# A state-space convolution block on one core: the opening's loads, biases, silus and weight folding in another order

## The chip, the cores and the metric

The kernel runs on one core of one Trainium2 chip. The metric is the device time of one execution in microseconds (us); lower is better. Three runs of the kernel before gave 1737.27 us as their median, from 1737.03 to 1740.41.

## The reference, cut to what matters

The input x has 4 images of 128 channels on 96 x 96 pixels. A group norm (32 groups of 4 channels) comes first. The normed image is then read as a sequence in four directions (rows, rows reversed, columns, columns reversed), and each sequence goes through the same layer; the four results are turned back, multiplied by the fuse weights and added to x.

```python
t = _grouped1x1(x, in_proj_w, in_proj_b, G)          # 128 -> 2 x 256 channels
u, gate = (t[:, :HID], t[:, HID:])
u = silu(u)
u = conv_general_dilated(u, dw_w, padding 2, 5 taps, depthwise)
...                                                  # s, a, bb, cc from u; a scan over the sequence
u = u + _conv1x1(cc * hst + ssm_d[None, :, None] * s, ssm_out_w)
u = _grouped1x1(u * sigmoid(gate), mix_w, mix_b, G)
return _conv1x1(u, out_proj_w, out_proj_b)
...
x = x + einsum('oc,bchw->bohw', fuse_w, y) + fuse_b
```

## The kernel before

The sequences are cut into steps of 16 lines; a step has 4 phases (the position modulo 4, called g or r in the code) and 2 directions s, and 256 hidden channels in two halves j. A *pair* is one phase of one step with both directions; `pair(t)` for t below 6 and `pair_on(t)` from there on make up nearly all of the program, 192 pairs in all. Nothing schedules the work: the instructions stand on each engine in the order in which the code is written, and semaphores are put in where one engine needs another's result. So an instruction that waits holds up all that stands behind it on its engine.

`start()` is the opening, before the first pair. It does the following.

- x of the first image comes in pieces into `acc` (`load_x`, L333 to L337). The image is counted in 24 chunks of 384 columns. As each piece lands, VectorE takes the statistics of its chunks (`bn_stats`, L337).
- While that goes on, TensorE runs fillers (L1188), matmuls whose result nobody reads, first three of 512 columns, then smaller ones, each behind a 6-column matmul (L1216) that waits for the statistics of one chunk.
- The generator `stats_first` (L176 to L216) turns the statistics into the norm. `bn_aggr` (L178); a small product over the groups gives the mean; `ex`; another gives the variance; ScalarE takes the square root (L198) and loads the table for silu (L200); L205 scales the input weights to `wn`. One more product and 16 tiny matmuls give the eight bias columns `bn` (L215, L216). Its `yield`s let `start` put other work between.
- `outer` (L1195) multiplies output weights by fuse weights for each of the four directions d and copies them to `w_of` (L1199). `inner` (L1203) multiplies in the mix weights and L1208 scales the result into `w_fin`. GpSimd then adds up `w_of` and `w_fuse` over the directions in place, four additions on L1257, here called **the fold**. Three one-column matmuls (L1281) use the folded weights, and ScalarE makes `b_fin` of them (L1282). The first addition of the fold overwrites the first two directions of `w_of`, so it waits for the first `inner`, which reads them; the third of the L1281 matmuls reads what the fourth addition writes.
- `burst(j, g)` is the input projection of one phase and half: per direction four 32 x 32 matmuls with 385 columns, from `x_in` through `wn` into a PSUM bank. `silus(j, g)` is its two ScalarE activations (L527) into the tile `sil`; memsets of `edges` (L487, L489) follow on VectorE.
- The second half of the hidden channels (j = 1) gets the 5-tap convolution by `taps`, on VectorE (L740, L744). The first half (j = 0) gets it by TensorE: `conv` (weights `band`) and `conv_less` (weights `less`), after which ScalarE copies the result to `u` (L717).
- The last thing in `start` are the three L1281 matmuls and `b_fin`. Then `pair(0)` begins with its `proj`: first the input projection of the next step for one phase (16 matmuls of 385 columns), then 16 matmuls from `u` through `main`, and so on.

PSUM has eight banks. `taps` work in banks 0 and 1; `banks` in `start` names the two banks of each burst; before, `outer` has the banks 0, 1, 4 and 5, one for each direction, and `inner` has 0 and 1.

SyncE's queue issues the loads in this order: ten pieces of x, the tile of output and fuse weights (`shared`, L353), `main` (L330; it holds the input weights that L205 reads), the two tiles `x_in` of the first step (L305), eight small ones for the gates (L323). All its DMAs take turns on eight semaphores, and an issue waits until the DMA that had its semaphore eight issues earlier has landed. So the eight L323 issues tell, one after the other, when the last four pieces of x, `shared`, `main` and the two `x_in` tiles landed (or SyncE came free).

## Time and profile before

| what | value |
|---|---|
| median of three runs | 1737.27 us (1737.03 to 1740.41) |
| profiled execution, first to last instruction (span) | 1735.2 us |
| median less span: what lies around the instructions | 2.07 us |
| TensorE busy in the span | 1713.6 us, 99% |
| VectorE, ScalarE, GpSimd busy | 1507.9, 1494.8, 1447.0 us |
| TensorE's first instruction starts | 11.66 us |
| silus of the opening: first one starts, last one ends | 24.46 us, 32.18 us |
| first matmul of `pair(0)` | 33.71 us |

The page of the profile gives busy times by engine, the chain of work that ended last, and the costliest groups. The timeline lists instructions in order of time, equal ones merged: start, duration of the group, engine, line, operation, output from input, and in brackets how long the engine had been idle and what released it. A matmul in fp32 stands there as two records. The windows give busy time and DMA rate by stretch of time.

### The profile page before, as it was taken

What the parts mean: (1) busy time and instruction counts of PE and PEld (TensorE: products, weight loads), DVE (VectorE), ACT (ScalarE), POOL (GpSimd) and SP (SyncE); (2) the same over time, 40 slices, a digit from 0 to 9 for tenths busy, and PEclk for the clock granted to TensorE, in tenths of its full rate; (3) what the DMA queues carried; (4) which work ended last, traced back from release to release, by engine and by line L of the source; (5) the groups of instructions that cost most, each with busy time, mean ns of one, the idle gap of its engine ahead of it and who ended that gap; (6) DMA issues with size and microseconds to landing.
All of it is one profiled execution on the core that took longest, in us unless ns stands there. A gap on an engine that the chain in (4) does not pass through costs nothing.

```text
span 1735.2 us, 54226 instructions
## 1 busy us (share of the span) xinstructions
PE 1713.6 (99%) x22522; PEld 644.7 (37%) x22522; DVE 1507.9 (87%) x1508; ACT 1494.8 (86%) x2544; POOL 1447.0 (83%) x1490
## 2 busy tenths in 40 slices
PE   7999999999999999999999999999999999999998
PEld 4333333343333433344333443334333333333333
DVE  6899998888889998888889999888888888888887
ACT  4888988889888888888988888888998889888875
POOL 3689889888789988888788988887878889887887
PEclk9999999999999999999999999999999999999999
DMA  7746865358884786337896487433887548643364
GB/s 244 235 147 218 288 202 151 124 206 280 275 287 139 262 267 194 118 126 263 260 308 226 150 300 251 144 123 132 294 294 239 179 144 304 201 137 133 147 226 166
DMA packets 154644, 363.66 MB, mean 210 GB/s; under 512 B 19104, under 2 KB 120864, under 8 KB 154400
## 3 DMA queue, kind: packets, MB, share of 16 engines
q1 hardware_dynamic: 154256, 360.16, 62.8%
q8 instruction: 178, 2.92, 0.7%
q14 instruction: 66, 0.54, 0.1%
q10 hardware_dynamic: 144, 0.04, 0.0%
HBM read 221.41 MB, written 138.53 MB: 207 GB/s over the span
## 4 chain that ended last, share of the span: by engine, by line
PE 95%; DVE 2%; ACT 1%; DMA 1%; issue 0%; SPq 0%; DVEq 0%; ACTq 0%
PE psum L130 81%; PE psum L577 8%; PE psum L557 5%; DVE psum L744 1%; PE psum L1188 0%; DMA acc<-in_xr 0%; DMA kept<-shared 0%; DVE u L638 0%; ACT psum L589 0%; ACT psum L742 0%; DVE u L744 0%; ACT sil L527 0%; SPq L335 0%; PE psum L1195 0%; DVE u L691 0%
## 5 line engine op out<-in xcount | busy, mean ns | idle before, releaser
L744 DVE SCALAR_TENSOR_TENSOR psum<-sil,small,psum 128x768 f32<-128x768 f32 x576 | 589.1, 1023 | 42.2 <-ACT psum L742 16.8
L130 PE MATMUL psum<-u,w_fin 128*32 128x384 f32 (+1 forms) x6192 | 541.3, 484 | 1.1 <-ACT ys L860 0.4
L130 PE MATMUL psum<-u,main 128*32 128x384 f32 x6144 | 535.0, 489 | 0.5 <-DVE u L691 0.4
L638 DVE SCALAR_TENSOR_TENSOR u<-gate,psum 128x768 f32<-128x768 f32 x376 | 341.7, 950 | 150.0 <-PE psum L577 50.8
L879 POOL TENSOR_TENSOR acc<-ys,acc 128x384 f32<-128x384 f32 x375 | 411.8, 1120 | 14.0 <-ACT ys L860 1.9
L825 POOL TENSOR_TENSOR t<-t,t 64x384 f32<-64x384 f32 (+1 forms) x192 | 287.2, 1496 | 70.6 <-DVE t L819 48.3
L589 ACT COPY psum<-u 128x768 f32<-128x768 f32 x384 | 301.4, 799 | 10.5 <-DVE u L638 4.3
L130 PEld LDWEIGHTS psum<-u,w_fin 128*32 128x32 f32 x6192 | 195.2, 109 | 309.6 <-issue 235.5
L130 PEld LDWEIGHTS psum<-u,main 128*32 128x32 f32 x6144 | 180.0, 109 | 324.5 <-issue 218.3
L130 PE MATMUL psum<-sil,band 128*32 128x384 f32 x3072 | 285.3, 488 | 0.0
L792 POOL TENSOR_SCALAR t<-tm 64x384 f32<-64x384 f32 x184 | 170.8, 928 | 114.4 <-ACT tm L781 102.4
L826 POOL TENSOR_TENSOR t<-t,t 64x384 f32<-64x384 f32 (+1 forms) x192 | 233.9, 1218 | 15.1
L793 POOL TENSOR_TENSOR t<-t,tm 64x384 f32<-64x384 f32 x192 | 213.8, 1113 | 30.2 <-ACT t L784 15.5
L577 PE MATMUL psum<-t,main 32*128 32x384 f32 x1536 | 228.1, 525 | 4.2 <-ACT psum L589 4.2
L742 ACT ACTIVATE psum<-sil,small 128x768 f32<-128x768 f32 x191 | 172.6, 904 | 65.2 <-DVE u L638 61.9
L744 DVE SCALAR_TENSOR_TENSOR u<-sil,small,psum 128x768 f32<-128x768 f32 x192 | 194.9, 1015 | 6.8
L527 ACT ACTIVATE sil<-psum,bnorm 128x385 f32<-128x385 f32 x384 | 191.6, 584 | 4.0 <-DMA edge<-sil 0.9
L557 PE MATMUL psum<-x_in,wn 32*128 32x384 f32 x768 | 161.7, 498 | 0.0
L862 ACT COPY ys<-psum 128x384 f32<-128x384 f32 x288 | 132.3, 478 | 33.0 <-PE psum L130 28.3
L130 PEld LDWEIGHTS psum<-sil,band 128*32 128x32 f32 x3072 | 88.8, 108 | 171.4 <-issue 63.1
L781 ACT ACTIVATE tm<-psum,small 128x384 f32<-128x384 f32 x192 | 110.9, 578 | 14.0 <-PE psum L130 2.3
L577 PEld LDWEIGHTS psum<-t,main 32*128 32x128 f32 x1536 | 93.9, 183 | 73.7 <-issue 41.0
(108 smaller groups left out, 1512.3 us busy)
## 6 DMA issues: line engine op xcount, KB each, us to landing
gate<-kept SPq DMA_DIRECT2D x114, 768.0 KB, 5.2
kept<-gate SPq DMA_DIRECT2D x74, 768.0 KB, 3.7
sil<-sil SPq DMA_DIRECT2D x64, 770.0 KB, 6.6
lone<-edge SPq DMA_DIRECT2D x40, 770.0 KB, 7.5
x_in<-in_xs SPq DMA_DIRECT2D x250, 96.2 KB, 3.3
edge<-sil SPq DMA_DIRECT2D x96, 192.5 KB, 3.6
out<-acc SPq DMA_DIRECT2D x46, 384.0 KB, 6.4
acc<-in_xr SPq DMA_DIRECT2D x39, 384.0 KB, 6.4
```

Source lines behind the costliest of these rows:

```text
L130: nc.tensor.matmul(o[r, : rhs.shape[-1]], lhsT, rhs, start=start, stop=stop, skip_group_check=True)
L527: nc.scalar.activation(sils[step][:, s, j, g, :], bank(bk)[:, : N + 1], AF.Silu, bias=bn[:, 1:2] if j else bn[:, 4 + g : 5 + g],)
L557: nc.tensor.matmul(bank(to)[:, :N], stats[un["b"]][0][r, s, :], x_in[s][r, q, off : off + N], start=True, stop=True)
L577: nc.tensor.matmul(bank(ssm(bi, s) + j)[:, :N], w_so[r, bass.ts(j, P)], z[r, :], start=(bi, s) not in seeded, stop=True, skip_group_check= ...
L589: nc.scalar.copy(psum[:, ssm(bi, s) : ssm(bi, s) + 2, :N], us[bi][:, s])
L638: nc.vector.scalar_tensor_tensor(v, g, 1.0, pz, ALU.add, ALU.mult)
L742: nc.scalar.activation(part, src, AF.Copy, scale=w_tap[:, 0:1])
L744: nc.vector.scalar_tensor_tensor(us[i][:, :, 1, :] if k == K - 1 else part, src, w_tap[:, k : k + 1], part, ALU.mult, ALU.add,)
L793: nc.gpsimd.tensor_mul(ta[0:64, p, :], tb[0:64, :], tm[0:64, :])
L825: engine.tensor_mul(ta[0:64, p, r], tb[64:P, r], ta[64:P, p, r])
L826: engine.tensor_add(tb[0:64, r], ta[0:64, p, r], tb[0:64, r])
L879: adder.tensor_add(part, y, part)
```

## The change

Ten things change, all in the opening; every pair after it is as before.

1. x comes in 15 pieces: three of one chunk, nine of two, three of one. Before, it came in ten of 1, 1, 1, 2, 2, 3, 4, 4, 4 and 2 chunks.
2. The fillers read the first 512 columns of x, not columns from chunk 10 on. There are five of 512 columns, then eight of 128, each behind a 6-column matmul on the statistics of one of the last eight chunks.
3. The four first bias columns are made by themselves (L212), ahead of the 16 tiny matmuls, which now write bank 7; the other four come by L217 after another `yield`. The first burst stands between the two.
4. `outer` runs in banks 4 and 5, two directions in each. Only direction 0 goes before the variance; the copies of the other three go to VectorE and stand behind all biases.
5. The bursts and silus of j = 1 come first, then those of j = 0.
6. The banks of the bursts are a ring of three pairs.
7. All taps of the first phase are spread between the silus of j = 1 and j = 0. Before, they lay behind the silus of j = 0.
8. `load_rows` reloads `x_in` for the next step in four issues, not eight.
9. `conv` and `conv_less` come after all silus. Before, they stood among the silus of j = 1.
10. `inner` and the fold come after `conv_less` and the edge DMAs, directly ahead of the L1281 matmuls (L1283 after the change). Before, they stood among the silus.

```diff
-        pb = bank(free[0])
+        pb, pg = bank(7), bank(7)[:, 4:8]
         product(pb[:, 0:4], wn, gm4)
+        nc.vector.tensor_sub(bn[:, 0:4], b_in[:, 0:4], pb[:, 0:4])
+        yield
         for g in range(4):
             for q in range(R):
-                mm(pb[:, 4 + g : 5 + g], q, ..., mean[0:32, :], True, True)
-        nc.vector.tensor_sub(bn, b_in, pb[:, 0:8])
+                mm(pg[:, g : g + 1], q, ..., mean[0:32, :], True, True)
+        nc.vector.tensor_sub(bn[:, 4:8], b_in[:, 4:8], pg[:, 0:4])
...
-    load_x([(0, 1), (1, 1), (2, 1), (3, 2), (5, 2), (7, 3), (10, 4), (14, 4), (18, 4), (22, 2)])
+    load_x([(0, 1), (1, 1), (2, 1)] + [(c, 2) for c in range(3, 21, 2)] + [(21, 1), (22, 1), (23, 1)])
...
-        for n in (512, 512, 512):
-            filler(n)
+        for i in (7, 7, 7, 0, 1):
+            filler(512, i)
         next(pieces)
-        for c, n in ((NSC - 5, 192), (NSC - 4, 192), (NSC - 3, 192), (NSC - 2, 192), (NSC - 1, 256)):
+        for c in range(NSC - 8, NSC):
...
-            filler(n)
+            filler(128)
         next(pieces)
-        outer(0, 0, nc.scalar.copy)
-        outer(1, 1, nc.scalar.copy)
+        outer(0, nc.scalar.copy)()
         next(pieces)
-        outer(2, 4, nc.scalar.copy)
+        copies = [outer(d, nc.vector.tensor_copy) for d in (1, 2, 3)]
         next(pieces)
-        outer(3, 5, nc.vector.tensor_copy)
-        filler(128)
+        sils[0] = new_sil(0)
+        pairs = {1: ((2, 3), (6, 7), (4, 5), (2, 3)), 0: ((6, 7), (4, 5), (2, 3), (6, 7))}
...
+        next(pieces)
+        burst(1, TURN[0])
         for _ in pieces:
             pass
-        for g in range(R):
-            burst(0, g)
+        for copy in copies:
+            copy()
+        burst(1, TURN[1])
+        burst(1, TURN[2])
+        new_u(0)
+        silus(1, TURN[0])
+        taps(0, (0,), nc.vector)
+        burst(1, TURN[3])
+        load_rows(1, slice(0, R))
...
         silus(0, 0)
-        burst(1, TURN[0])
-        silus(0, 1)
-        burst(1, TURN[1])
-        silus(0, 2)
-        inner((0, 1), 0)
-        inner((2, 3), 1)
+        burst(0, 3)
+        load_rows(0, slice(0, R))
+        for g in range(1, R):
+            silus(0, g)
+        conv(0, head_banks(0))
+        conv_less(0, head_banks(0))
+        keep_lone(0)
+        load_lone(0)
+        inner((0, 1), 2)
+        inner((2, 3), 3)
         for w in (w_of, w_fuse):
             for e in (2, 1):
                 nc.gpsimd.tensor_add(w[:, 0:e], w[:, 0:e], w[:, e : 2 * e])
...
         pf = bank(3)
```

The built programs show the places. On TensorE, at the end of the opening, before (`x_in_70` and `x_in_71` are the two directions' inputs, L1203 is `inner`, L1281 the three one-column matmuls that wait for the fold, and the x_in rows behind them are the first of `pair(0)`):

```order
L1203 MATMUL psum<-shared 128x128 x8
L130 MATMUL psum<-x_in_70,wn_269 32x385 x4
L130 MATMUL psum<-x_in_71,wn_269 32x385 x4
L130 MATMUL psum<-x_in_70,wn_269 32x385 x4
L130 MATMUL psum<-x_in_71,wn_269 32x385 x4
L130 MATMUL psum<-sil_299,band 32x384 x8
L130 MATMUL psum<-sil_299,less 32x384 x8
L1281 MATMUL psum<-small,shared 128x1 x3
L130 MATMUL psum<-x_in_70,wn_269 32x385 x8
L130 MATMUL psum<-x_in_71,wn_269 32x385 x8
```

The same place on TensorE after the change (L1205 is `inner`, L1283 the one-column matmuls):

```order
L130 MATMUL psum<-sil_286,band 32x384 x8
L130 MATMUL psum<-sil_286,less 32x384 x8
L1205 MATMUL psum<-shared 128x128 x8
L1283 MATMUL psum<-small,shared 128x1 x3
L130 MATMUL psum<-x_in_70,wn_282 32x385 x8
L130 MATMUL psum<-x_in_71,wn_282 32x385 x8
L130 MATMUL psum<-u_0_1_0_337,main 32x384 x16
```

Between `inner` and the one-column matmuls there stood two bursts, `conv` and `conv_less`; now nothing stands between them. On VectorE, from the bias columns to the first taps, before (L215 and L216 are the biases, L1199 the one copy of `outer` that VectorE had, L1208 the scaling behind `inner`):

```order
L1199 COPY shared<-psum 128x256
L215 TENSOR_TENSOR bnorm_272<-small,psum 128x8
L216 TENSOR_SCALAR bnorm_272<-bnorm_272 128x2
L487 MEMSET sil_299 64x1 x6
L1208 TENSOR_SCALAR w_fin<-psum 128x512 x2
L487 MEMSET sil_299 64x1 x2
L489 MEMSET sil_299 128x2
L740 TENSOR_SCALAR psum<-sil_299,small 128x2x384
```

And on VectorE after the change, from the biases to the scaling behind `inner`, all numbers of lines moved by one or two:

```order
L212 TENSOR_TENSOR bnorm_285<-small,psum 128x4
L217 TENSOR_TENSOR bnorm_285<-small,psum 128x4
L218 TENSOR_SCALAR bnorm_285<-bnorm_285 128x2
L1201 COPY shared<-psum 128x256 x3
L491 MEMSET sil_286 128x2
L742 TENSOR_SCALAR psum<-sil_286,small 128x2x384
L746 SCALAR_TENSOR_TENSOR psum<-sil_286,small,psum 128x2x384 x2
L491 MEMSET sil_286 128x2
L746 SCALAR_TENSOR_TENSOR psum<-sil_286,small,psum 128x2x384
L746 SCALAR_TENSOR_TENSOR u_0_1_0_337<-sil_286,small,psum 128x2x384
L489 MEMSET sil_286 64x1 x8
L1210 TENSOR_SCALAR w_fin<-psum 128x512 x2
```

Three copies now stand behind the biases, and the taps of the first phase stand ahead of the j = 0 memsets and of the scaling. The third burst (banks 4 and 5) waits for the second and third of these copies.

More of the change, by code (lines that the diff above doesn't have):

```diff
@@ L1244, in load_rows @@
                 load_front(1, s, slice(64 * s + 32 * j, 64 * s + 32 * j + 32), r)
-        for g in range(R):
-            burst(0, g)
-        silus(0, 0)
-        burst(1, TURN[0])
-        silus(0, 1)
-        burst(1, TURN[1])
-        silus(0, 2)
-        inner((0, 1), 0)
-        inner((2, 3), 1)
+        next(pieces)
+        burst(1, TURN[0])
+        for _ in pieces:
+            pass
+        for copy in copies:
[7 more added lines that the diff above has]
+        load_rows(1, slice(0, R))
+        silus(1, TURN[1])
+        taps(0, (1,))
+        burst(0, 0)
+        silus(1, TURN[2])
+        taps(0, (2,))
+        burst(0, 1)
+        silus(1, TURN[3])
+        taps(0, (3, 4))
+        burst(0, 2)
+        silus(0, 0)
+        burst(0, 3)
[8 more added lines that the diff above has]
+        inner((2, 3), 3)
         for w in (w_of, w_fuse):
```

44 lines of the change are left out of this document (11 added, 33 removed).

## The prediction

> **What bounds the kernel now.** I read the page first: the engines' busy times.
>
> ```profile
> span 1735.2 us, 54226 instructions
> PE 1713.6 (99%) x22522; PEld 644.7 (37%) x22522; DVE 1507.9 (87%) x1508; ACT 1494.8 (86%) x2544; POOL 1447.0 (83%) x1490
> ```
>
> TensorE is idle for 21.6 us in all. So whatever moves its work of the pairs to earlier or later moves the end by as much, unless an idle stretch takes it up. The change touches only what lies ahead of the pairs; I therefore look for one moment: when TensorE starts its first matmul of `pair(0)`. Next comes the chain of waits (start, length, what); in the opening it runs through TensorE from its first filler on.
>
> ```profile
> 11.66 5.49 PE psum L1188 x6
> ...
> 19.29 0.43 PE psum L1188 x2
> ```
>
> But a TensorE that always has a record may still be paced by others, so I read the timelines of TensorE, VectorE, ScalarE and GpSimd (start, length, group, idle time before it).
>
> ```profile
> 20.30 0.24 PE L130 MATMUL psum<-mv,gmean 128*32 128x1 f32 x8
> 20.48 1.16 PE L1195 MATMUL psum<-shared 128*128 128x128 f32 x8
> 21.56 0.31 PE L130 MATMUL psum<-ex,gmean 128*32 128x1 f32 x16
> ...
> 23.29 0.43 PE L130 MATMUL psum<-mean,wn 32*32 32x1 f32 x32
> 23.56 3.80 PE L130 MATMUL psum<-x_in,wn 32*32 32x385 f32 x96
> 27.29 2.05 PE L1203 MATMUL psum<-shared 128*128 128x128 f32 x16
> ...
> 30.72 1.50 PE L130 MATMUL psum<-sil,band 128*32 128x384 f32 x16
> ...
> 32.95 0.83 PE L1281 MATMUL psum<-small,shared 128*128 128x1 f32 x6
> 33.71 1.28 PE L130 MATMUL psum<-x_in,wn 32*32 32x385 f32 x32
> ```
>
> ```profile
> 18.33 0.81 DVE L178 BATCH_NORM_AGGREGATE mv<-bn 128x2 f32<-128x144 f32 x1
> 20.61 0.16 DVE L183 COPY mean<-psum 128x1 f32<-128x1 f32 x1 [1.48 <-PE psum L130]
> ...
> 21.00 0.22 DVE L187 SCALAR_TENSOR_TENSOR ex<-dev,mv 128x1 f32<-128x1 f32 x1
> ...
> 22.57 0.48 DVE L205 TENSOR_SCALAR wn<-main,inv 128x128 f32<-128x128 f32 x2
> 22.99 0.42 DVE L1199 COPY shared<-psum 128x256 f32<-128x256 f32 x1
> ```
>
> ```profile
> 24.46 7.72 ACT L527 ACTIVATE sil<-psum,bnorm 128x385 f32<-128x385 f32 x16 [0.34 <-PE psum L130]
> ...
> 35.85 0.91 ACT L742 ACTIVATE psum<-sil,small 128x768 f32<-128x768 f32 x1 [0.16 <-DVE u L744]
> ```
>
> ```profile
> 28.59 3.31 POOL L1257 TENSOR_TENSOR shared<-shared 128x512 f32<-128x512 f32 x4 [8.42 <-PE psum L1203]
> ```
>
> From 24.46 to 32.18 us ScalarE sets the pace: 16 silus, 0.48 us apart, without a gap. `inner` (2.05 us) and the fold (3.31 us) lie under them, and the fold ends at 31.90, before TensorE asks for its result at 32.95. From 33.71 on the pairs run.
>
> **The change, part by part.** *The arrival of x and `x_in`.* SyncE's small gate loads tell the landings. The third and fourth are in the first row below; each takes 0.47 us, so the fourth starts at 16.41, when the last piece of x has landed. The eighth, in the second row, starts when `x_in_71` has landed, at 23.18. Behind them stand rates in windows of one microsecond: busy time of five engines, clock, DMA share, GB/s.
>
> ```profile
> 15.43 1.45 SPq L323 DMA_DIRECT2D x_in<-in_xs  x2
> ```
>
> ```profile
> 23.18 0.47 SPq L323 DMA_DIRECT2D x_in<-in_xs  x1
> ```
>
> ```profile
> 3.00:4.00 1.00, 0.00 (x0) 0.00 (x0) 0.47 (x1) 0.00 (x0) 0.84 (x5) 1.00 0.81 244
> ...
> 6.00:7.00 1.00, 0.00 (x0) 0.00 (x0) 0.63 (x2) 0.00 (x0) 0.84 (x3) 1.00 1.06 378
> ...
> 12.00:13.00 1.00, 1.00 (x2) 0.48 (x2) 1.00 (x3) 0.00 (x0) 0.00 (x0) 1.00 1.02 424
> ...
> 14.00:15.00 1.00, 1.00 (x2) 0.34 (x1) 1.00 (x4) 0.00 (x0) 0.00 (x0) 1.00 1.04 419
> ```
>
> A chunk is 0.197 MB. Up to chunk 6 the pieces are the same. Behind it 17 chunks now come as seven pieces of two and three of one, where mostly pieces of four came. At 424 GB/s, the rate while pieces of four moved, 17 chunks take 7.9 us. Pieces of two ran at 378 (6 to 7 us) to 419 (14 to 15 us), pieces of one at 244 with the engines busy 0.81 of the time, so 301. At 419 and 301 the 17 chunks take 8.5 us, at 378 and 301 9.2 us. If size does not matter, nothing is lost; nothing can be gained either, as the same bytes stand ahead of `x_in`. So `x_in` lands 0 to 1.4 us later. I take 0.7, near the 419 of a two-chunk piece with a full queue: the last x at 17.1, `x_in_71` at 23.9.
>
> *The norm.* One `bn_stats` stands behind the last landing; the row of x's tile gives its length.
>
> ```profile
> L337 DVE BATCH_NORM_STATS2 bn<-acc x24: 541/544/561, 3.5 to 17.8; 128x6 f32<-128x384 f32 x24
> ```
>
> Now VectorE is still working off pieces of four when x has landed, and `bn_aggr` starts at 18.33. Then it would start at 17.1 + 0.55 = 17.65 and end at 18.5. The mean's product follows at once: TensorE's fillers, which held it up to 20.30 (VectorE idle 1.48), have been worked through while x came. They now start at about 4 us instead of 11.66 and hide behind the statistics; without that cover the last of them would cost 0.2. From the product to `wn` it is 2.75 us in the row (20.30 to 23.05), less the 0.34 for which the next product waited behind `outer` (21.22 to 21.56): `wn` at 20.9. The six matmuls of `outer` that now follow the variance (0.87 of the row's 1.16) end at about 21.2. TensorE could begin the first burst at 21.4, 2.1 us earlier than 23.56. **But the data is not there**: the burst's second direction needs `x_in_71`, at 23.9. First silu 0.90 behind its burst (23.56 to 24.46): the second silu starts at 24.8, against 24.94. Of 2.1 us, 0.1 is left.
>
> *Biases and copies.* The 16 tiny matmuls (0.43) stand behind that burst; then VectorE makes the other biases (two of 0.16) and three copies of 0.42. Second and third copy end at 25.6 and 26.0. The third burst waits for them, so its silus, the fifth and sixth, start at 26.55 and 27.0 instead of 26.25 and 26.7. I take 0.3 lost, 0 to 0.6 by the landing. The last ten silus follow at 0.48: the silus end at 32.3, against 32.18.
>
> *Taps, banks, reloads.* The taps go under the silus: VectorE has nothing else there. The reload of `x_in` for `pair(0)` can start when the last j = 0 burst is through, about 30.5, and such loads took 4.0 us.
>
> ```profile
> x_in<-in_xs SPq DMA_DIRECT2D x2, 192.5 KB, 4.0
> ```
>
> That is there by 35, well before its use below. I count both at nothing; a later landing shows only beyond 39.
>
> *`conv`, `inner`, the fold.* This is the term that counts. `conv` can start one silu before the last, at 31.85; from its start to the one-column matmuls it took 2.23 us (30.72 to 32.95), so `conv_less` ends at 34.1, 1.15 later than before. Then comes `inner`. The fold started 1.30 us behind `inner`'s start (27.29 to 28.59), so at 35.4, and takes 3.31: 38.7. The third one-column matmul waits for it, and behind it in TensorE's order wait all matmuls of `pair(0)`, 0.28 later (a third of 0.83): **39.0, against 33.71**. Taken apart: 4.9 us between `conv_less` and `pair(0)` instead of 0.76, and 1.15 from what lies ahead. `inner` and the fold lost their cover, the silus, and TensorE, which runs through now, would stand still from 36.1 (end of `inner`) to 38.7. GpSimd's durations are taken from the same four additions.
>
> *What the pairs give back.* ScalarE's first tap waited 0.16 for the taps that are now long done. The ceiling is TensorE's idle time in the first pairs:
>
> ```profile
> 33.70:95.10 61.40, 59.55 (x829) 19.95 (x832) 53.79 (x58) 50.67 (x92) 34.52 (x33) 1.00 0.73 228
> ```
>
> 1.85 us in 61.4. I take 0.5, nearer to the wait that I can name; the ends are 0.16 and 1.85.
>
> **Sum:** +5.3 - 0.5 = +4.8 us on the span of 1735.2: 1740.0. The median is 2.07 above that span, so 1742.1 us. The ends: landing 0 to 1.4 instead of 0.7 (-0.7 to +0.7), copies (-0.3 to +0.3), given back 0.16 to 1.85 (+0.35 to -1.35). All at once give +2.5 to +6.1; two of them rarely add up fully.
>
> **A rule against the change: the clock.** The fillers show it: 3 x 512 columns took 5.49 us in six records, 1.79 ns a column, and later 2 x 192 columns 0.43 us, 1.12 ns. TensorE thus ran slow for its first 5.5 us, though the rows' granted clock (the 1.00 ahead of the DMA share) says 1.00 all along. If the hole of 2.6 us ahead of `pair(0)` made it slow again for 5.5 us, this would cost 5.5 x (1 - 1.12/1.79) = 2.1 us. [...]
>
> **The rivals.**
> 1. *The hole is given back whole by the idle time, 1.85 us, or somewhat more*: +2.5 to +3.4, about 1740.2. For it: "busy" holds modelled ends, so the pairs may have slack that no row shows. Against: VectorE and ScalarE cannot work ahead, as each pair's work on them begins with TensorE's product.
> 2. *Not slower: the pairs are paced by SyncE's chain of loads.* If TensorE in the first pairs in truth follows edge, lone and `x_in` loads, which start at the end of the silus, then its start does not count as long as it is earlier than the loads allow. Silus end at the same time (+0.1), and four reload issues fewer, about 0.42 us each, bring that chain forward by up to 1.7: about 1736.0. It decides if the slack of those loads is over 5 us. Against: TensorE never waits for a DMA between 33.7 and 95.1, and is idle 1.85 us there.
> 3. *The clock falls in the hole*: +2.1, 1744.2.
> 4. *It does not do what it says*: small pieces bring x later by the full 1.4 us, the norm gains 0.1 instead of 0.7, `x_in_71` comes at 24.6: 1742.8.
>
> **How the numbers follow.** The forecast has 0.66, the rivals 0.11, 0.07, 0.09 and 0.07. The forecast's own ends, 1740.4 to 1743.4, hold most of it; to leave out no more than 2 in 10 the range goes from 1739.4 (inside rival 1) to 1744.2 (rival 3). A measurement tells 0.2%, 3.5 us, from no change: the bounds are 1740.7 and 1733.8. Slower: rivals 3 and 4 and nine tenths of the forecast, 0.76. Same: the rest of the forecast, rival 1 and most of rival 2, 0.21. Faster: 0.03.
>
> **What would show it.** In the profile of the changed kernel: `bn_aggr` near 17.7; a burst whose second half starts at about 23.9 with TensorE idle before it, released by the DMA of `x_in`; silus ending near 32.3; the fold's group on GpSimd from 35.4 to 38.7; TensorE idle up to 38.7, released by GpSimd; `pair(0)` at 39.0. The prediction is wrong if `pair(0)` starts by 35, if the pairs behind it draw more than 1.9 us closer than before, or if the first pairs' matmuls run at 1.8 ns a column.

## The result, and the profile after

The changed kernel takes **1748.68 us** (median of 5 executions, 1746.91 to 1749.84) against 1737.27 (5 executions, 1736.70 to 1740.41): a ratio of 1.0062, 95% interval 1.0050 to 1.0074. It is slower, as forecast, but by 11.4 us instead of 4.8, and it lies above the range's end of 1744.2. The busy shares on the page give no hint of the cause, as TensorE stays at 99%; but it is busy 13.4 us longer, with 14 records more, in a span that is 12.6 us longer.

```profile
span 1747.8 us, 54255 instructions
PE 1727.0 (99%) x22536; PEld 653.3 (37%) x22536; DVE 1508.5 (86%) x1511; ACT 1495.9 (86%) x2542; POOL 1447.9 (83%) x1490
```

The windows tell where to look (start:end and length, busy time and count of five engines, then granted clock, DMA share, GB/s). In this profile the clock changes at 7.25, 14.08 and 41.39 us, 6.83 and 27.31 us apart; the borders are these moments and others at multiples of 3.41 us from them.

```profile
7.25:10.66 3.41, 3.05 (x7) 1.02 (x6) 3.16 (x8) 0.00 (x0) 3.10 (x9) 1.00 1.02 393
10.67:14.08 3.41, 0.00 (x0) 0.00 (x0) 3.41 (x9) 0.00 (x0) 0.50 (x2) 1.00 1.03 404
14.09:27.73 13.64, 13.57 (x124) 12.01 (x127) 5.82 (x18) 2.16 (x5) 0.39 (x1) 0.50 0.83 218
27.74:41.38 13.64, 13.41 (x160) 6.36 (x158) 6.74 (x20) 8.40 (x17) 0.00 (x0) 0.50 0.40 109
41.40:44.80 3.40, 2.03 (x19) 1.84 (x17) 1.38 (x2) 0.45 (x1) 2.32 (x3) 1.00 0.30 63
```

From 14.08 to 41.39 us TensorE's granted clock is 0.50. Before, the same column says 1.00 all through the opening, though the first fillers ran slow there by their rate (1.79 ns a column against 1.12 later), as the prediction read. The timeline of TensorE shows what stands ahead of it, and what it does to the steps of the forecast (start, length, engine, line, work; lines in the tail of the code are numbered two higher than before).

```profile
4.31 5.99 PE L1190 MATMUL psum<-acc 128*128 128x512 f32 x10 [4.31 <-DMA acc<-in_xr]
14.16 0.59 PE L1218 MATMUL psum<-bn,acc 128*128 128x6 f32 x2 [3.87 <-DVE bn L339]
...
21.29 0.29 PE L130 MATMUL psum<-mv,gmean 128*32 128x1 f32 x8
...
25.84 0.29 PE L130 MATMUL psum<-gm,wn 128*32 128x4 f32 x8
26.06 0.89 PE L130 MATMUL psum<-x_in,wn 32*32 32x385 f32 x8
...
36.64 2.84 PE L130 MATMUL psum<-sil,band 128*32 128x384 f32 x16 [0.23 <-issue]
39.41 1.53 PE L130 MATMUL psum<-sil,less 64*32 64x384 f32 x16
40.87 2.28 PE L1205 MATMUL psum<-shared 128*128 128x128 f32 x16
44.52 0.61 PE L1283 MATMUL psum<-small,shared 128*128 128x1 f32 x4 [1.37 <-POOL shared L1279]
45.74 0.38 PE L1283 MATMUL psum<-small,shared 128*128 128x1 f32 x2 [0.61 <-POOL shared L1279]
46.05 1.27 PE L130 MATMUL psum<-x_in,wn 32*32 32x385 f32 x32
```

The five fillers of 512 columns run as soon as chunk 0 is there, and are through at 10.3. Then TensorE is idle for 3.87 us, until the statistics of chunk 16. Right behind, at half clock, eight steps of 6 and 128 columns take 0.86 us each and hold the mean's product up to 21.29, though its input was there by 18.3. VectorE, ScalarE and GpSimd show the rest.

```profile
17.50 0.80 DVE L178 BATCH_NORM_AGGREGATE mv<-bn 128x2 f32<-128x144 f32 x1
21.64 0.16 DVE L183 COPY mean<-psum 128x1 f32<-128x1 f32 x1 [3.34 <-PE psum L130]
```

```profile
27.63 1.05 ACT L529 ACTIVATE sil<-psum,bnorm 128x385 f32<-128x385 f32 x2 [2.60 <-PE psum L130]
...
35.96 1.07 ACT L529 ACTIVATE sil<-psum,bnorm 128x385 f32<-128x385 f32 x2 [0.16 <-PE psum L130]
```

```profile
42.40 3.28 POOL L1279 TENSOR_TENSOR shared<-shared 128x512 f32<-128x512 f32 x4 [21.91 <-PE psum L1205]
```

| moment | before | forecast | after |
|---|---|---|---|
| mean's product | 20.30 | 18.5 | 21.29 |
| silus end | 32.18 | 32.3 | 37.03 |
| `conv_less` done, next work of TensorE | 32.95 | 34.1 | 40.87 |
| `pair(0)` | 33.71 | 39.0 | 46.05 |

From there on everything keeps its distance: the product of `u` and `main` in the second pair starts at 53.99 instead of 41.82, 12.17 later, and the whole span is 12.6 longer. The profile is of the longest of the five executions (1749.84 us, mean clock 0.992); two others have a mean clock of 0.995 and 0.996, by an estimate (twice what is missing from 1, times the span) 17 and 14 us of half clock instead of 27.3, and take 1747.34 and 1746.91 us.

### The profile page after: what moved, and what is told of

Same layout as the page of the kernel before. It is cut to its first block, busy times and chain, and to the rows that moved or that the text cites. A ratio compares the mean times of both kernels' runs of the same rounds, so it can differ in the third digit from the quotient of the medians.

```text
span 1747.8 us, 54255 instructions
## 1 busy us (share of the span) xinstructions
PE 1727.0 (99%) x22536; PEld 653.3 (37%) x22536; DVE 1508.5 (86%) x1511; ACT 1495.9 (86%) x2542; POOL 1447.9 (83%) x1490
## 4 chain that ended last, share of the span: by engine, by line
PE 95%; DVE 2%; ACT 1%; DMA 1%; issue 1%; POOL 0%; SPq 0%; DVEq 0%; ACTq 0%; POOLq 0%
PE psum L130 81%; PE psum L579 8%; PE psum L559 5%; DVE psum L746 1%; DMA kept<-shared 0%; DVE bn L339 0%; DVE u L640 0%; DMA acc<-in_xr 0%; ACT psum L591 0%; PE psum L1190 0%; ACT psum L744 0%; DVE u L746 0%; PE psum L1197 0%; POOL shared L1279 0%; ACT sil L529 0%
## 5 line engine op out<-in xcount | busy, mean ns | idle before, releaser
L783 ACT ACTIVATE tm<-psum,small 128x384 f32<-128x384 f32 x192 | 111.2, 579 | 14.3 <-PE psum L130 4.1
```

## The experiments

The theory behind them changed once. At first: the clock fell because of the idle 3.87 us, and the rest of the loss is the fold. The first four runs showed that this is too narrow, since with the hole filled the clock fell in other places, and from then on it reads: **in these kernels the clock falls where little of TensorE's array streams for some 3.4 us (0.17 of it in a_ten, 0.24 in a_thin, against 0.46 in a_bridge, where it held), idle or not, and the new order has several such places**. All ratios are to the kernel before on the same chip.

**a_bridge: TensorE gets work in the hole.**

```diff
-        for c in range(NSC - 8, NSC):
+        for c in range(NSC - 16, NSC):
```

> The changed kernel, with the step of a 6-column matmul and a 128-column filler made behind each of the chunks 8 to 23 instead of 16 to 23, so that TensorE has work between 10.3 and 14.2 us, where it was idle for 3.87 us. Theory (the clock fell in that hole, and the rest of the loss is the fold): granted clock 1.00 throughout, mean's product near 18.5 instead of 21.29, silus end near 32.5 instead of 37.03, fold still behind conv_less, pair(0) at 39 to 39.5, about 1742. Rival (128 columns a chunk are too little work to hold the clock, hole or not): the clock still falls to 0.5 ahead of 20 us, pair(0) at 45 to 46, about 1748. Rival (the loss is in the loads of x and x_in): first silu of the second half no earlier than after, time within 2 us of 1748.7.

Measured 1749.1 us (1746.62 to 1750.5), ratio 1.0065 (1.0053 to 1.0078): nothing gained. The hole is gone, the mean's product comes at 19.28, and the clock holds through the fillers; but it falls at 26.5, in the bursts, and is back only at 40.1. `pair(0)` starts at 44.49, 1.56 earlier than in the changed kernel, but the clock has fallen again at 43.5, behind the wait for the fold, and is low up to 50.4, which takes that gain away. The rival on the loads fails by its own sign: the first silu starts at 24.43 instead of 27.63.

**a_ten: before's fillers in the changed kernel** (chunk 10, three of 512 columns, five steps).

```diff
-                bank(i)[:, :n], accf[:, 0:P], accf[:, 0:n], start=True, stop=True
+                bank(i)[:, :n], accf[:, bass.ds(10 * SC, P)], accf[:, bass.ds(10 * SC, n)],
+                start=True, stop=True,
...
-        for i in (7, 7, 7, 0, 1):
+        for i in (7, 0, 1):
...
-        for c in range(NSC - 8, NSC):
+        for c in range(NSC - 5, NSC):
```

> The changed kernel with before's fillers: on chunk 10, three of 512 columns, then steps behind the last five chunks (still 128 columns each). TensorE starts at 11.7 and has no hole. Theory (clock in the hole plus fold): half speed until about 17, then full; mean's product 18.6 to 19.0, silus end 32.4, fold 35.5 to 38.8, pair(0) at 39.1, about 1742. Rival (thin fillers of 128 let the clock fall): granted 0.5 somewhere from 17 to 41, about 1746 to 1748.

Measured 1747.48 us (1745.55 to 1747.6), 1.0051 (1.0038 to 1.0065). No early hole, and the clock falls all the same, three times. Its windows, cut where it changes:

```profile
16.59:26.82 10.23, 8.84 (x137) 5.94 (x140) 5.38 (x20) 3.85 (x8) 0.41 (x1) 1.00 0.81 198
26.83:30.23 3.40, 3.40 (x62) 1.80 (x61) 3.06 (x3) 2.72 (x6) 0.00 (x0) 0.50 0.01 1
30.24:33.64 3.40, 1.87 (x42) 0.70 (x27) 2.33 (x10) 3.40 (x9) 0.00 (x0) 1.00 0.60 143
33.66:37.05 3.39, 3.37 (x24) 1.04 (x32) 0.09 (x2) 0.39 (x1) 0.00 (x0) 0.50 0.70 206
37.07:43.88 6.81, 4.83 (x74) 3.20 (x62) 1.38 (x2) 1.56 (x4) 3.13 (x4) 1.00 0.55 176
43.90:47.29 3.39, 3.39 (x24) 1.09 (x20) 1.99 (x2) 2.31 (x5) 0.00 (x0) 0.50 0.15 34
```

The stretches between the changes are 3.4, 6.8 and 10.2 us long: in this profile every one is 3.41 us or twice or three times as much. Each fall follows a stretch that holds one of the idle places which the new order made. TensorE's rows name them:

```profile
22.69 0.85 PE L130 MATMUL psum<-x_in,wn 32*32 32x385 f32 x8 [0.50 <-DMA x_in<-in_xs]
24.35 0.53 PE L130 MATMUL psum<-x_in,wn 32*32 32x385 f32 x4 [0.81 <-DMA x_in<-in_xs]
...
33.68 2.84 PE L130 MATMUL psum<-sil,band 128*32 128x384 f32 x16 [1.56 <-ACT sil L529]
...
40.94 0.61 PE L1284 MATMUL psum<-small,shared 128*128 128x1 f32 x4 [1.37 <-POOL shared L1280]
```

The wait for `x_in`, the wait of `conv` for the last silus, and the wait for the fold. The longest, for the fold, has 1.98 us, in two pieces of 1.37 and 0.61.

**a_fold and a_both: `inner` and the fold back under the silus**, in the changed kernel and together with a_bridge.

```diff
         burst(1, TURN[2])
+        inner((0, 1), 0)
+        inner((2, 3), 1)
+        for w in (w_of, w_fuse):
+            for e in (2, 1):
+                nc.gpsimd.tensor_add(w[:, 0:e], w[:, 0:e], w[:, e : 2 * e])
         new_u(0)
...
-        inner((0, 1), 2)
-        inner((2, 3), 3)
-        for w in (w_of, w_fuse):
-            for e in (2, 1):
-                nc.gpsimd.tensor_add(w[:, 0:e], w[:, 0:e], w[:, e : 2 * e])
```

> The changed kernel with inner and the fold behind the third burst of the second half (banks 0 and 1), everything else as changed, so the clock still halves from 15 to 41. Theory (both losses add; at half clock TensorE is what the silus wait for, so inner's work there takes about 4 us of what the moved fold gives): conv_less ends 41 to 45 and pair(0) follows it by 1 to 1.5; pair(0) at 42 to 46, about 1744.5 to 1748. Rival (only the fold counts, the clock costs nothing): pair(0) near 41, 1743 or less.

> Bridge and early fold together. Theory: clock 1.00, inner under the silus, fold ends near 31 to 32, silus end 32.4 to 32.6, conv_less ends 34.2, pair(0) at 34.9, given back 0.3: about 1738, 0.7 above before. Rival (something else of the change costs too: copies, biases, taps, late rows): 1740 or more with pair(0) later than 36.

Measured 1748.46 (1.0064, 1.0051 to 1.0076) and 1747.64 us (1.0057, 1.0045 to 1.0070); for a_both about 1738 had been expected. The fold no longer holds anyone up, but a new wait stands in its place. In a_both, TensorE, then VectorE:

```profile
37.63 3.37 PE L130 MATMUL psum<-sil,band 128*32 128x384 f32 x16 [2.59 <-DVE sil L489]
```

```profile
31.33 0.69 DVE L1210 TENSOR_SCALAR w_fin<-psum 128x512 f32<-128x512 f32 x1 [0.66 <-PE psum L1205]
...
37.41 0.89 DVE L489 MEMSET sil<- 64x1 f32 x8
```

The scalings out of `inner`'s banks (L1210) keep the taps from these banks to 32.0; the memsets of the first half stand behind the taps, and `conv` waits for the memsets. The clock fell in both kernels besides: by the windows of their profiles it is at 0.50 from 14.3 to 34.8 and from 41.6 to 45.0 us in a_fold, from 27.4 to 30.8 and from 37.6 to 41.0 in a_both.

**a_thin: is it idleness?** a_bridge with 64 columns instead of 128 in each step; TensorE is as seldom idle.

```diff
-            filler(128)
+            filler(64)
```

> a_bridge with 64 instead of 128 columns in each of its 16 steps: TensorE then streams about 0.24 of its array instead of 0.47 in the stretch of 10 to 18 us, yet is never idle for longer than 0.3 us in one piece. Theory (the clock goes by how much of the array streams in a stretch of 3.4 us): granted clock 0.5 from 13 to 18 us on. Rival (it goes by an idle stretch of some 3.4 us alone): 1.00 up to 20 us at least, as in a_bridge.

Measured 1747.69 us (2 executions). The clock falls at 15.06. The stretch ahead of the fall in a_thin, and one at the same place in a_bridge:

```profile
11.64:15.05 3.41, 3.41 (x30) 3.39 (x29) 3.41 (x8) 0.00 (x0) 0.00 (x0) 1.00 1.05 397
```

```profile
12.82:16.23 3.41, 3.41 (x31) 3.39 (x30) 3.41 (x8) 0.00 (x0) 0.00 (x0) 1.00 1.04 389
```

Both times TensorE is busy all 3.41 us by the profile, whose ends of matmuls are modelled, and the clock falls in the one and stays in the other. So idle time, as far as the profile shows it, did not decide here. What differs is how much streams. In a_warm2 below, 2560 columns in six records go from 40.11 to the next start at 42.26, so 0.84 ns a column at full clock. Seven steps of two records of 64 and two of 6 are 980 columns, 0.82 us, **0.24** of the stretch; with 128 it is 1876 columns, **0.46**. Counting a 32 x 32 tile as a sixteenth of the fillers' 128 x 128, the stretch ahead of a_ten's first fall (28 records of 385 columns, 32 of one) streams 0.17. These shares are estimates, from the records that begin in a stretch and the 0.84 ns.

The same estimate for the changed kernel, in stretches of 3.41 us from 10.67 on: 0 ahead of the fall; then at half clock, where a column is counted double, 0.46, 0.53, 0.70, 0.57, 0.63, 0.58 and 0.64, behind each of which the clock stayed low; and 0.74 in the one behind which it came back, at 41.39. In a_ten it came back at 30.24 behind bursts alone, 62 records of 385 columns by the window's count of all that run in it; in the changed kernel 69, from 31.15 to 34.56, did not bring it back. So the share is no sharp measure. In the profile of before, no 3.41 us that begin between 12 and 54 us stream less than 0.47, what runs up to 17.80 counted double for its slow rate; the clock there holds to the end of the opening.

**a_warm, a_warm2, a_warm3: fill the thin places of a_ten.** In a_warm2 with 512 columns ahead of each half of the first burst, 126 ahead of each later burst, 512 + 384 ahead of `conv`, 512 + 512 + 256 under the fold; a_warm has fewer columns in the first burst and fillers behind the bursts; a_warm3 has fillers at three later bursts only, and smaller ones.

```diff
+            if (j, g) in ((1, TURN[3]), (0, 1), (0, 3)):   # a_warm3
+                spare(spots[j, g][0])                      # 126 columns
             for s in range(2):
+                if (j, g) == (1, TURN[0]):
+                    filler((512, 256)[s], s)
                 in_proj(0, g, s, j, spots[j, g][s])
...
+        filler(512, 4)
+        filler(192, 5)
         conv(0, head_banks(0))
...
+        for n in (512, 512, 256):
+            filler(n, 5)
         pf = bank(3)
```

> a_ten with extra fillers in TensorE's idle places: a 126-column one behind each burst in the unused columns of its bank, two inside the first burst, three ahead of conv, and 2 x 512 + 256 columns between inner and the one-column matmuls. Theory now (TensorE is clocked down wherever it streams too little of its array within a stretch of 3.4 us, and four places of the new order are that thin; the other terms hold): granted clock 1.00 from 17 on, silus end 33.3 to 33.7 instead of 34.05, conv and conv_less in 2.3 to 2.5 us instead of 3.84, pair(0) at 39.3 to 40.3 instead of 42.47, first proj 2.8 instead of 4.48 us: 1742 to 1743. Rival (the loss behind 24 us is not the clock but waits for banks and copies): within 1 us of a_ten's 1747.5.

> a_ten with fillers in its three thin places, none of them behind a burst: 512 columns ahead of each half of the first burst (while x_in is awaited), 126 ahead of each later burst, 512 + 384 ahead of conv, 512 + 512 + 256 between inner and the one-column matmuls. Theory (what a_ten loses behind 24 us is the lowered clock, which comes wherever TensorE streams under about a third of its array in a stretch of 3.4 us): granted clock 1.00 from 17 on in most executions, silus end 33.0 to 33.5, conv and conv_less in 2.3 to 2.5 us, pair(0) at 39.7 to 40.5, first proj in 2.8 us: about 1743. Rival (waits, not the clock): 1747 or more, with the clock at 1.00 all the same.

> a_warm2 with its fillers thinned so that they stop slowing the bursts: 512 and 256 columns ahead of the halves of the first burst, 126 ahead of three of the other seven bursts instead of all, 512 + 192 ahead of conv, 512 + 512 + 256 under the fold. Theory A (forecast's sum holds at full clock, plus 0.3 to 0.8 for x_in that lands later): clock 1.00 from 17 on, pair(0) at 40 to 41, 1742 to 1743. Theory B (order and fold cost more than forecast, clock apart): clock 1.00 and pair(0) at 42 or later, 1744 or more.

a_warm: 1755.74 us, 1.0091 (1.0074 to 1.0108). A miss that teaches: the clock fell at 26.7 with the first burst still too thin, and then the fillers themselves kept TensorE late; the half clock stayed for 20.5 us (a burst took 1.53 us instead of a_warm2's 0.88), through bursts of 16 records with two of 126 columns every 2.19 us, an estimated share of 0.49. a_warm2: 1747.14 us, 1.0064 (1.0051 to 1.0076). The profiled execution has the clock at 1.00 from 17 to 45 us, yet its fillers cost as much as they save: a burst and its filler take 1.22 us, where two silus take 0.96, and silus end at 35.45. Four of its five executions have a mean clock of 1.000 and take 1746.49 to 1747.83, 9.3 to 10.7 over before: the rival's time, with the clock up as the rival had it. The last steps of its TensorE:

```profile
40.11 2.31 PE L1190 MATMUL psum<-acc 128*128 128x512 f32 x6
42.26 0.98 PE L1297 MATMUL psum<-small,shared 128*128 128x1 f32 x6
43.17 1.27 PE L130 MATMUL psum<-x_in,wn 32*32 32x385 f32 x32
```

a_warm3, with fewer fillers, separates the two, since its executions fall into two groups. Four have a mean clock of 0.999 or 1.000 and take **1743.03 to 1744.39 us**; four have 0.996 and take **1749.75 to 1750.51**. The profile is one of the latter:

```profile
26.86:40.48 13.62, 13.62 (x118) 4.59 (x114) 5.47 (x14) 6.70 (x13) 0.00 (x0) 0.50 0.30 84
```

The same program, then, with and without 13.6 us of half clock: 6.3 us apart in the groups' means (for the faster group, which has no profile, the mean clock says so). At full clock, order and fold cost 6.4 to 7.7 over before's 1736.67 in these runs, its fillers' cost included. Three of the four lie between the two theories' numbers (1743 and 1744) and one within B's, so neither is confirmed.

**a_defer and a_warm_defer: nobody waits for the fold.** The one-column matmuls and `b_fin` go behind `pair(0)`, in a_ten, and in a_warm2 without its last fillers.

```diff
-        start()
+        late = start()
         for t in range(LAG):
             pair(t)
+            if t == 0:
+                late()
```

> a_ten with the one-column matmuls and b_fin moved behind pair(0), so that no matmul waits for the fold, which runs beside pair(0). Fold term as forecast: 2.6 to 3.3 us earlier than a_ten, pair(0) near 39.5 instead of 42.47. Theory of the clock: the thin stretch of 38 to 41 us goes too, so the first proj runs in 2.8 instead of 4.48 us, another 1.7: about 1742.5 to 1743.5 in all. Rival (the pairs take up what the fold costs): 1746 or more.

> Both: the fillers of a_warm2 up to conv, and the one-column matmuls behind pair(0). Theory: clock 1.00 from 17 on, silus end 33.0 to 33.5, pair(0) at about 37.3: 1740 to 1741, what remains being inner's 2.05 us without cover and the later silus. Rival: as a_defer.

Measured 1746.15 (1.0053, 1.0039 to 1.0066) and 1745.98 us (1.0057, 1.0045 to 1.0070). In the profile of a_defer, `pair(0)` starts 2.57 behind `inner`'s start (38.65 to 41.22) instead of 4.95 in a_ten (37.52 to 42.47); but the clock fell at 26.3 and was low to 39.9, so that `conv` came 0.74 later than in a_ten, and ahead of the second pair the one-column matmuls (0.83) now stand and TensorE waits 0.81 for `b_fin`. It gains 1.3 us where 4 to 5 were expected, and the rival's number came (1746 or more). In a_warm_defer this is not the clock: four of its five executions have a mean clock of 1.000 and take 1745.09 to 1746.63, where 1740 to 1741 were expected. Moving the wait mostly moves its cost; where the rest of that time lies is open, as the profile is of the fifth execution (1752.11, mean clock 0.996).

**b_fill0, b_late, b_pieces: one part of the change in the kernel before.** Fillers on chunk 0; `inner` and the fold behind `conv_less`; the smaller pieces of x.

```diff
-                bank(7)[:, :n], accf[:, bass.ds(10 * SC, P)], accf[:, bass.ds(10 * SC, n)],
+                bank(7)[:, :n], accf[:, 0:P], accf[:, 0:n],                    # b_fill0
...
-        inner((0, 1), 0)
-        inner((2, 3), 1)
...
+        inner((0, 1), 2)                                                       # b_late
+        inner((2, 3), 3)
+        for w in (w_of, w_fuse):
+            for e in (2, 1):
+                nc.gpsimd.tensor_add(w[:, 0:e], w[:, 0:e], w[:, e : 2 * e])
         pf = bank(3)
...
-    load_x([(0, 1), (1, 1), (2, 1), (3, 2), (5, 2), (7, 3), (10, 4), (14, 4), (18, 4), (22, 2)])
+    load_x([(0, 1), (1, 1), (2, 1)] + [(c, 2) for c in range(3, 21, 2)] + [(21, 1), (22, 1), (23, 1)])
```

> The kernel before with its fillers reading chunk 0 instead of 10, nothing else. Theory: they run at 4.3 to about 8, TensorE is then idle to about 17, the clock falls by 14 and, as bursts alone bring it back hardly if at all, stays low up to conv; 1741 to 1746. Rival (an early start is free, the statistics hide it): 1737.

> The kernel before with inner and the fold moved behind conv_less (banks 2 and 3), nothing else. Fold term as forecast: pair(0) about 4.1 later than 33.71, at 37.8, 1741 with the clock at 1.00. Theory (the hole of 2 us under the fold is thin enough for the gate in some executions): 1741 to 1743.5, granted clock 0.5 for one stretch of 3.4 us in some runs. Rival (given back whole by idle time in the pairs): 1738 or less.

> The kernel before with the changed kernel's pieces of x, nothing else. Forecast's term: x and x_in land 0 to 1.4 later, bn_aggr at 17.6 to 18.3, fillers as before hold the mean's product to 20.3; silus end at most 0.7 later: 1737 to 1738. Rival (small pieces cost more): 1739 and above.

b_fill0: **1746.25 us** (12 executions, 1740.07 to 1747.39), 1.0037 (1.0025 to 1.0049). Starting the fillers early, by itself, costs most of what the whole change costs: 8.7 us in the medians, 6.4 by the ratio, which also counts the four executions of 1740.07 to 1743.03, whose mean clock is 0.995 or 0.996 against 0.991 and 0.992 of the other eight. Its hole is longer than the changed kernel's, 8.23 us (8.94 to 17.17), as the wide fillers are three and the steps begin at chunk 19. In its profile (mean clock 0.992) the clock is at 0.50 from 11.46 to 38.76, through all six bursts of this row and 3.2 us of `inner`, which take 6.99 and 3.57 us; before, the same rows took 3.80 and 2.05:

```profile
28.64 6.99 PE L130 MATMUL psum<-x_in,wn 32*32 32x385 f32 x96
35.55 3.57 PE L1203 MATMUL psum<-shared 128*128 128x128 f32 x16
...
43.50 1.28 PE L130 MATMUL psum<-x_in,wn 32*32 32x385 f32 x32
```

b_late: 1742.93 us (12 executions), 1.0021 (1.0008 to 1.0033). Sorted by the execution's mean clock it reads like a price list: 1738.85 at 1.000, 1741.07 and 1741.89 at 0.999, 1741.94 to 1743.35 at 0.998, 1743.60 to 1744.85 at 0.997, 1745.85 and 1746.08 at 0.996. b_pieces: 1739.54 us (12 executions), 1.0006 (0.9993 to 1.0019): a cost of the pieces cannot be told from nothing, nor from the forecast's 0.7 us, as the interval reaches 3.3 us. The median is the rival's (1739 and above), the profiled execution (1737.05) the forecast's; six of the twelve have a mean clock of 0.996 to 0.998. In the profile `x_in` makes TensorE wait for 0.45 up to 24.08.

**b_late_warm and a_early: the fold alone and the order alone, thin places filled.** b_late_warm has 126 columns ahead of each burst of the second half and 512 + 512 + 256 under the fold. a_early is a_ten with `inner` and the fold as in a_fold, a_warm3's fillers at the first burst and ahead of `conv`, and the first half's memsets on GpSimd.

```diff
-            edges(0, g, j, nc.vector)
+            edges(0, g, j, nc.vector if j else nc.gpsimd)   # a_early
```

> b_late with 126 columns of filler ahead of each of the four bursts of the second half (in the TensorE time that inner left) and 512 + 512 + 256 under the fold, so that no stretch of 3.4 us is thin. Forecast's fold term alone: clock 1.00, pair(0) at 37.5 to 38, 1741 to 1741.5, and no execution above 1742.5, against b_late's 1738.85 to 1746.08. Rival (the fold itself costs about 2, as b_late's fastest execution has it): 1738.5 to 1739.5.

> The changed order without its two costs: before's fillers, inner and the fold behind the third burst (as a_fold), the first half's edge memsets on GpSimd so that conv does not wait for VectorE's taps, fillers of 512 and 256 ahead of the halves of the first burst and 512 + 192 ahead of conv. What is left is the order of the halves itself. Theory: clock mostly 1.00, conv near 34, pair(0) at 36 to 37, 1739.5 to 1740.5. Rival (the order costs nothing by itself): 1737 to 1738.

b_late_warm: 1741.60 us, 1.0034 (1.0021 to 1.0048). Eight executions with a clock of 0.999 or 1.000 take 1739.72 to 1741.87, 3.1 to 5.2 over before, its fillers' cost included: the fold's term, forecast at 4.1, fits. Against it stands one execution of b_late, 1738.85 at 1.000, only 1.3 over that session's median of before; it has no profile. The other four (0.996) take 1747.45 to 1747.80; here too the half clock stayed under the fillers, from 26.42 to 40.05. My "no execution above 1742.5" was wrong. a_early: 1742.39 us, 1.0027 (1.0016 to 1.0037); its four executions at 1.000 take 1740.47 to 1740.83, 3.8 to 4.2 over before. So the rest of the changed order costs about 4 us with the fold covered and the clock up, a_early's own fillers and its place for `inner` included; what the order of the halves costs alone is not separated. `pair(0)` starts at 38.29, where 36 to 37 had been expected. ScalarE and TensorE show by what:

```profile
27.66 1.05 ACT L529 ACTIVATE sil<-psum,bnorm 128x385 f32<-128x385 f32 x2 [0.16 <-PE psum L130]
30.75 4.83 ACT L529 ACTIVATE sil<-psum,bnorm 128x385 f32<-128x385 f32 x10 [2.04 <-PE psum L130]
```

```profile
35.26 1.53 PE L130 MATMUL psum<-sil,band 128*32 128x384 f32 x16 [0.22 <-POOL sil L489]
```

`inner`, ahead of the fourth burst, makes the silus wait for 2.04 us, and `conv` still needs the first half's last memsets; before, `conv` ran under the second half's silus.

**b_guard: a version to beat both.** The kernel before, with steps of 128 columns, and 512 columns where `x_in` is awaited.

```diff
-(NSC - 5, 192), (NSC - 4, 192), (NSC - 3, 192), (NSC - 2, 192), (NSC - 1, 256)
+(NSC - 5, 128), (NSC - 4, 128), (NSC - 3, 128), (NSC - 2, 128), (NSC - 1, 128)
...
+        nc.tensor.matmul(
+            bank(2), accf[:, bass.ds(10 * SC, P)], accf[:, bass.ds(10 * SC, 512)],
+            start=True, stop=True,
+        )
         sils[0] = new_sil(0)
```

> The kernel before with five steps of 128 columns instead of 192 and 256, and one filler of 512 columns ahead of the first burst, where x_in is awaited. Theory (before's executions of 1741 to 1744 are those in which the clock fell in that wait): median 1736.5 to 1737.5, clock 1.000 in all executions, none above 1739. Rival (those executions have another cause): the same spread as before, or slower by the filler's 0.9.

Measured 1737.07 us, 0.9999 (0.9989 to 1.0008): the same. Its 11 executions lie between 1736.14 and 1738.12, those of before on the same chip between 1735.34 and 1746.08, but only 2 of these 32 are above 1740, so that 11 without one prove little. No version here beats the kernel before. That before's longer executions are those with a lowered clock does show: in the runs beside b_fill0, the 22 of 29 with a mean clock of 0.999 or 1.000 take up to 1738.64, the 7 with 0.996 to 0.998 take 1741.07 to 1744.27.

## Why the prediction was right in direction and wrong in size

**The step that failed** is what the prediction says of TensorE's fillers: "They now start at about 4 us instead of 11.66 and hide behind the statistics; without that cover the last of them would cost 0.2." The fillers were costed as work, and as work they are hidden. Their purpose was left out: to have the clock up when the opening's real matmuls come. Started at 4.3 they are spent at 10.3, and the clock is gone at 14.08. b_fill0, the early start alone and with a longer hole, costs 8.7 us in the medians (1746.25 against 1737.59).

**The clock was weighed, but only at one hole.** I looked at the 2.6 us ahead of `pair(0)`, and gave the fall there a chance of 0.09 and a price of 2.1. That the clock would rather hold there was my estimate, and no run shows it: in a_bridge and a_ten it fell at 43.5 and 43.9, behind this wait with its 1.98 us of idle time. The hole ahead of the fall in the changed kernel was another, of 3.87 us. At the rates that the prediction worked out (1.79 ns a column for 5.5 us, then 1.12) the five fillers would have ended near 12.1, some 2 us ahead of the statistics of chunk 16, so that the working already held a hole that I did not look for; they then reached full clock after 2.9 us (4.31 to 7.25) and ended at 10.3. The length of an idle place does not tell the falls either: 3.87 us stand ahead of the changed kernel's, but a_thin loses the clock behind a stretch without any idle time in the profile, and a_ten's three falls follow idle places of at most 1.98 us.

**The price of a fall was mis-sized.** I put it at one warm-up, 5.5 us of slower fillers. In the changed kernel's profile the bursts, 32 x 32 tiles, reach a share of 0.58 to 0.63 at half clock, the clock stayed low behind them, and it came back behind 0.74, at the end of `conv` and `conv_less`; in that of b_fill0 it stayed low up to `inner`. The half clock lasted 27.3 us in both. a_warm3's two groups give 6.3 us for 13.6 us of it; the changed kernel's own executions give only 1.3 to 2.9 us for an estimated 10 to 13 us, so the price is not the same everywhere. The rates were read too close together as well: the 1.12 ns a column held the gaps between small fillers, where a_warm2's wide ones take 0.84, so that 5.5 us at half clock would have cost 5.5 x 0.5 = 2.75 and not 2.1.

**The other terms, point by point.**
- *Statistics*: `bn_aggr` at 17.50, forecast 17.65. Right, but its gain went to the half-speed fillers.
- *`x_in`*: forecast 23.9. In the traces where TensorE waits for it, it comes at 24.08 (b_pieces), 24.35 (a_ten) and up to 24.68 (a_bridge); mis-sized by 0.2 to 0.8, at most 0.1 past the upper bound given (23.18 + 1.4). The idle time before it, released by the DMA, shows in a_ten as foretold.
- *`outer`*: the "six matmuls" were put at 0.87, as if a matmul were one record; they are 12 records, 1.60 us at full clock in a_ten (20.41 to 22.01). This cost nothing, since `x_in` was awaited behind them anyway.
- *Silus*: the second burst stands behind the tiny matmuls, which I had charged to the third burst's copies alone. In a_ten the second silu starts at 25.26 and the third at 26.19, 0.93 apart instead of 0.48: another 0.45.
- *Fold without cover*: 4.9 us between `conv_less` and `pair(0)` forecast; 5.18 in the changed kernel (40.87 to 46.05), and 3.1 to 5.2 in the time by b_late_warm. About right.
- *Given back*: 0.5 forecast, 0.17 measured (12.34 at the start of `pair(0)`, 12.17 in the second pair), the lower end. Behind that the pairs run at a fixed distance.
- *Taps and reload at nothing*: right for the changed order; the taps do cost when something delays them, as the memsets behind them in a_both show.

So at full clock, with a_ten's times, the sum would have been 4.8 + 0.45 + 0.45 + 0.33 = 6.0 us, and a_warm3 measured 6.4 to 7.7 with its own fillers in it. The rest of the 11.4, 3.7 to 5.0 us, is put down to the clock by subtraction; no run takes the low clock out of the changed kernel and leaves all else as it is. The parts do not add up (b_fill0's 8.7 and these 6.0 would make 14.7). That b_fill0's hole is longer, and that in the changed kernel `inner` no longer competes with the bursts while the clock is low, would account for it, but this is argued, not shown. How much of a_warm3's excess over 6.0 is its fillers stays open, as its profile is of an execution that lost the clock. Of the rivals, "the clock falls" named the mechanism, in the wrong place and at about half of its price. "Small pieces land late by the full 1.4 us" had the landing of `x_in` about right (24.6 foretold; 24.60 in a_early, 24.68 in a_bridge) and the norm wrong (`bn_aggr` at 17.50). "Paced by SyncE's chain" found nothing in its favour.

## What to carry to other kernels

Cost filler matmuls by what they keep up, not only by what they take: in these profiles the clock fell behind 3.41 us in which an estimated 0, 0.17 or 0.24 of the array streamed (columns x tile; the changed kernel, a_ten, a_thin) and held behind 0.46 (a_bridge). So when a change starts fillers earlier, shortens them or adds a wait behind them, ask what fills the time up to the next dense work. Work taken out from under another engine's time cost about its full length here, and more in the executions in which the hole also brought the clock down (b_late). And where executions of one kernel differ, sort them by their mean clock first: here that turned a scatter of 7 us into two tight groups.

## What the runs showed of the hardware

- The changes of the granted clock, between 1.00 and 0.50, lay 3.41 us or a multiple of it apart: 3.4, 6.8 and 10.2 us in a_ten, 10.2 in a_thin, 13.6 in a_bridge, a_warm3 and b_late_warm, 20.5 in a_fold, 6.83 and 27.31 in the changed kernel. Where they fall differs from execution to execution: in the profiles of a_bridge and a_both, alike up to there, the first fall is at 26.47 and 27.36.
- By the estimated shares, it fell behind 0 (the changed kernel, from 10.67), 0.17 (a_ten, from 23.41) and 0.24 (a_thin, from 11.64) and held behind 0.46 (a_bridge, from 12.82). At half clock it stayed low behind 0.46 to 0.70 in the changed kernel, and came back behind 0.74. So a fall outlasted its cause here: the changed kernel's, behind 3.87 us of idle time, lasted 27.31 us, and in a_warm, with fillers that made TensorE late, one lasted 20.5.
- Bursts of 32 x 32 tiles alone held the clock in before, at 96 records of 385 columns in 3.73 us (0.52, from 23.56). In a_ten it was lost at 28 of them in 3.41 us (0.17, from 23.41), with 0.81 us of waiting for `x_in` among them. At half clock bursts alone brought it back in a_ten (62 records that run between 26.83 and 30.23) and not in the changed kernel (69 between 31.15 and 34.56).
